# Graph and expert layers on one Trainium2 core: the steps between layers are written tile by tile over three engines, and the member tables become bf16

## The chip, the cores and the metric

The kernel runs on one core of one Trainium2 chip. The time is device microseconds (us) from the start to the end of the program. It was taken three times; the median is the figure that a change is held against. One more execution was recorded by the profiler; every duration below is of that execution.

## The reference

x has 3125 rows of 256 columns. Four pairs of a graph layer and a layer of experts are added to it, each fed with a layer norm of x:

```python
x = x + L0_gnn(layernorm(x), edge_index, edge_weight, ...)   # sums over 100000 edges, then relu(h @ W1 + b1) @ W2 + b2
x = x + L0_ffn(layernorm(x), router_w, w1, b1, w2, b2)       # tokens + the two best of 8 experts, gelu
x = x + L1_gnn(layernorm(x), edge_index, edge_attr_2, ...)   # attention over the edges, 4 heads
x = x + L1_ffn(layernorm(x), Wr, br, ln_g, ln_b, ...)        # router on the rows, experts on layernorm(rows)
x = x + L2_gnn(layernorm(x), W, a_src, a_dst, ..., bias)     # scores (h * a_src).sum per head, softmax per destination
x = x + L2_ffn(layernorm(x), Wg, bg, ...)                    # the two best of 8 experts, relu
x = x + L3_gnn(layernorm(x), W, b, src, dst)                 # three hops
x = x + L3_ffn(layernorm(x), gate_w, gate_b, ...)            # one expert of 8, with a capacity
```

A layer of experts takes logits = rows @ router, picks the best one or two experts for each row, sends the row through them (two products with an activation between) and adds the weighted answers. layernorm subtracts the mean of a row and divides by sqrt(variance + 1e-5).

## The kernel before

x stays in SBUF as 25 tiles of 128 rows, a tile `self.x` of 128 x 25 x 256 f32 (the last tile is partly filled). The stages follow each other as functions: `gcn`, `moe(0)`, `attention`, `moe(1)`, `gat`, `moe(2)`, `hops`, `switch`. The edges were sorted on the chip before. Long loops (the edge sums, the groups of 256 tokens of the experts) fill most of the span. Between two such loops lies a **step between layers**, and this change is about those.

Such a step has up to four parts, each a loop over the 25 tiles. First, x is completed: `gcn` multiplies by W2 (`ps_o`, L1238) and adds to x (L1240); `moe` reads back the experts' answers (`y`) and adds two of them a tile with weights m1 and m2 (L1571); `attention` multiplies its sums by a reciprocal (L1759) and adds them to x (L1760); `gat` does the same from DRAM (loads of `kept` and `sums`, L2259 to L2265). Second, `layernorm` takes bn_stats (L157) and bn_aggr (L160) of each tile on VectorE (DVE), once for each five tiles the root on ScalarE (ACT, L141) and the reciprocal (L142), and then subtracts and multiplies on DVE (L150). Third, `transposed` turns each tile by two transposes on TensorE (PE, L180, tile `ps_tr`), and `copy` takes the result out of PSUM, by turns on ACT (L172) and DVE (L170). Fourth, `logits` multiplies by 8 columns of the router (L1251), or the graph layer multiplies by its weights: attention 136 columns (L1628) and a copy to its table, gat 256 columns (L1866), from which ACT and DVE make two halves of a row (`hr`, L1872, L1873) and a table row `ts` (L1875), and DVE makes the source score by a product with a_src (L1878) and a sum over each head (L1879). In gat one operation then adds the bias to all of x (L1884), and x is written to `kept` (L1886).

Within one straight stretch of code the compiler's scheduler mixes these loops on an engine as it likes; a branch on a value (as in the expert loops) ends a stretch. Only in blocks called `in_order` do instructions of the engines named keep the order in which they are written.

After the logits comes the **routing**: probabilities and the best two (`pair_of_probs`, `pair_of_scores`), then `slots`, which numbers the tokens of each expert and ends in `members`. `members` builds one-hot tables by comparing numbers with `iota` (f32): `sl_ol` with 128 values for each of 25 tiles (L1401) and `sl_oj` with J = 64 values (L1404), multiplied by the tile's number (L1406) and by the partition's (L1408). Tables of the first and the second choice are built one after the other; for each tile one matmul (L1412) multiplies `sl_ol` with `sl_oj`, and `sl_tok` and `sl_to` (L1426) come out: which token sits in which slot. `expert_of` gives each group its expert (`sl_eid`). The experts wait for these. `moe(0)` also adds its normalised rows to x (L1543), and `moe(1)` calls `layernorm` a second time, on the normalised rows, after the logits.

Of the kernel before, what the change touches and what calls it, by code (L numbers as in the profile page):

```python
# [15 lines left out]
OP = mybir.AluOpType  # L16
# [72 lines left out]
class Net:  # L89
# [84 lines left out]
    def transposed(self, src, dst, psum, n=NT):  # L174

        nc = self.nc
        for t in range(n):
            ps = psum.tile([P, 2, P], F32, name="ps_tr", bufs=2)
            for k in range(2):
                nc.tensor.transpose(ps[:, k, :], src[:, t, k * P : (k + 1) * P], self.ident)  # L180
            self.copy(t, dst[:, :, t * P : (t + 1) * P], ps)

# [990 lines left out]
    def gcn_inputs(self):  # L1173
# [4 lines left out]
        if True:  # L1178
# [3 lines left out]
            w2 = keep.tile([P, 2, D], F32, name="w2")  # L1182
            loads.append(nc.sync.dma_start(out=w2, in_=a["L0_gnn_W2"].rearrange("(k p) f -> p k f", p=P)))
# [9 lines left out]
            self.first_inputs = w1, w2, bc, y  # L1193
            self.before_build = {SP: loads, DVE: ready}

    def gcn(self):
        nc, tc = self.nc, self.tc
        w1, w2, bc, y = self.first_inputs
        with self.l0:
            with tc.tile_pool(name="l0h", bufs=1) as hp, \  # L1200
# [3 lines left out]
                gT = hp.tile([P, 2, NT * P], F32, name="hT")  # L1204
# [30 lines left out]
                for t in range(NT):  # L1235
                    ps = psum.tile([P, D], F32, name="ps_o")
                    for f in range(2):
                        nc.tensor.matmul(ps, gT[:, f, t * P : (t + 1) * P], w2[:, f, :],  # L1238
                                         start=f == 0, stop=f == 1)
                    nc.vector.tensor_tensor(self.x[:, t, :], self.x[:, t, :], ps, op=OP.add)  # L1240


    def logits(self, pool, psum, xT, rw, bias):
# [5 lines left out]
        for t in range(NT):  # L1249
            for k in range(2):  # L1250
                nc.tensor.matmul(ps[:, t, :], xT[:, k, t * P : (t + 1) * P], rws[:, k, :],  # L1251
                                 start=k == 0, stop=k == 1)
        if bias is None:
            nc.vector.tensor_copy(lg, ps)
        else:
            bb = pool.tile([P, NE], F32, name="rb")
            nc.sync.dma_start(out=bb, in_=row_bcast(bias, NE))
            nc.vector.tensor_tensor(lg, ps, bb[:, None, :].to_broadcast([P, NT, NE]), op=OP.add)
        return lg
# [60 lines left out]
    def slots(self, pool, keep, psum, oh1, oh2):  # L1320
# [44 lines left out]
        tok, to = self.members(pool, keep, psum, slot, NG)  # L1365
        eid = self.expert_of(pool, keep, first, gf, NG)
        return tok, to, eid
# [14 lines left out]
    def members(self, pool, keep, psum, slot, n):  # L1382

        nc = self.nc
        k = slot.shape[1]

# [7 lines left out]
        ljf = pool.tile([P, 2, k * NT], F32, name="sl_lj")  # L1394
        nc.vector.tensor_copy(ljf, lj)
        ol = pool.tile([P, k * NT, P], BF16, name="sl_ol")
        oj = pool.tile([P, k, NT, 3, J], BF16, name="sl_oj")
        pt = psum.tile([P, 3, J], F32, name="ps_tok", bufs=1)
        for i in range(k):
            h = slice(i * NT, (i + 1) * NT)  # L1400
            nc.vector.tensor_tensor(ol[:, h], self.iota[:, None, :].to_broadcast([P, NT, P]),  # L1401
                                    ljf[:, 0, h, None].to_broadcast([P, NT, P]), op=OP.is_equal)
            o = oj[:, i]
            nc.vector.tensor_tensor(o[:, :, 2, :], self.iota[:, None, :J].to_broadcast([P, NT, J]),  # L1404
                                    ljf[:, 1, h, None].to_broadcast([P, NT, J]), op=OP.is_equal)
            nc.vector.tensor_tensor(o[:, :, 1, :], o[:, :, 2, :],  # L1406
                                    self.iota[:, :NT, None].to_broadcast([P, NT, J]), op=OP.mult)
            nc.vector.tensor_scalar(o[:, :, 0, :], o[:, :, 2, :], self.pidx, None, op0=OP.mult)  # L1408
            if i == 1:
                nc.vector.tensor_scalar(o[:, :, 2, :], o[:, :, 2, :], 2.0, None, op0=OP.mult)  # L1410
            for t in range(NT):
                nc.tensor.matmul(pt.rearrange("p v j -> p (v j)"), ol[:, i * NT + t, :],  # L1412
                                 o[:, t].rearrange("p v j -> p (v j)"),
# [15 lines left out]
    def experts(self, eid, tok, to, xrows, ybuf, pre, b, F, act, usual, scale_shift=None, gated=False):  # L1429
# [7 lines left out]
        with ExitStack() as st:  # L1437
# [61 lines left out]
            for u in range(usual[0]):  # L1499
                group(u)  # L1500
            n = nc.values_load(eid[0:1, usual[-1] :], min_val=0, max_val=usual[-1])
# [26 lines left out]
    def moe(self, layer):  # L1528
        nc, tc, a = self.nc, self.tc, self.a
        with ExitStack() as st:  # L1530

            xp = st.enter_context(tc.tile_pool(name="ex", bufs=1, side="right"))
            xrows, ybuf = self.xrows[layer], self.ybuf[layer]
            with tc.tile_pool(name="exn", bufs=1) as np_, \
                    tc.tile_pool(name="exps", bufs=2, space=PSUM) as psum:
                xn = np_.tile([P, NT, D], F32, name="xn")
                self.layernorm(self.x, xn)
                xT = np_.tile([P, 2, NT * P], F32, name="xT")
                self.transposed(xn, xT, psum)
                if layer == 0:  # L1540
                    lg = self.logits(np_, psum, xT, a["L0_ffn_router_w"], None)
                    m1, oh1, m2, oh2 = self.pair_of_probs(xp, lg)
# [1007 lines left out]
```

## Time and profile before

| what | value |
|---|---|
| median of three runs | 6228.87 us (6225.47 to 6233.80) |
| the profiled execution's own time | 6224.29 us |
| its span, first to last instruction | 6222.4 us |
| mean granted clock of PE | 0.858 |
| PE, DVE, ACT, POOL busy | 79%, 61%, 36%, 39% of the span |
| gcn: last product to logits | 1734 to 1796 us |
| combine after moe(0), attention's table | 1992 to 2051 us |
| attention's finish to logits | 2955 to 3018 us |
| combine after moe(1), gat's table | 3508 to 3611 us |
| gat's finish to logits | 4731 to 4801 us |
| switch: layer norm to logits | 5879 to 5925 us |
| the four routings | 1796 to 1832, 3018 to 3063, 4802 to 4835, 5925 to 5948 us |

Times inside the span count from its start. The profile gives for each engine its busy time; a matmul of f32 counts as two passes, each with a load of weights (PEld) of its own. In the timeline one row is one or several equal instructions on one engine: start, duration, engine, line, operation, what is written and read, and in brackets how long the engine was idle before, and what ended that. A clock of 1.00 is full speed of PE.

### The profile page before, as it was taken

The page shows a single profiled execution, that of the slowest core. Times are in us where ns is not written, and L with a number is a line of the kernel's source. Part 1 is how long each engine was busy: PE and PEld are TensorE (multiplying, and loading weights), DVE is VectorE, ACT ScalarE, POOL GpSimd, SP SyncE. Part 2 cuts the span into 40 slices and gives each one's busy share as a digit, 9 for nine tenths or more (in the row PEclk, how much of TensorE's full clock was granted, in tenths as well). Part 3 has the DMA queues.
Part 4 walks back from the last instruction along what each step waited for, and adds up shares of the span by engine and source line. Part 5 has one row for each costly group of instructions (what it writes and reads, how often), then busy time and mean ns, then how long its engine had stood idle before and what let it go on. Part 6 is the DMA issues. An engine that isn't in the chain of part 4 may idle for free. (4 is left out here: it accounts for less than half of the span.)

```text
span 6222.4 us, 89124 instructions
## 1 busy us (share of the span) xinstructions
PE 4939.7 (79%) x24912; PEld 3986.5 (64%) x24912; DVE 3771.5 (61%) x7790; ACT 2265.3 (36%) x5768; POOL 2425.1 (39%) x2329
## 2 busy tenths in 40 slices
PE   5446787568967888999499579999894899699886
PEld 4335776567855777777488445555554787588765
DVE  6788998681153898999511458888887100532343
ACT  3455776560012113444122166666660222110021
POOL 3778777740015563000022157777770222000021
PEclk8657777668978999999699779999996999899888
DMA  3482334456427574222355377777762554788653
GB/s 87 99 19 36 69 96 108 123 148 166 135 85 215 165 209 143 75 76 68 104 179 184 127 214 196 198 200 198 201 197 74 198 183 143 199 240 239 165 181 126
DMA packets 987149, 912.53 MB, mean 147 GB/s; under 512 B 188419, under 2 KB 897509, under 8 KB 985718
## 3 DMA queue, kind: packets, MB, share of 16 engines
q1 hardware_dynamic: 872098, 711.72, 40.5%
q0 software_dynamic: 84736, 166.99, 11.1%
q10 hardware_dynamic: 29764, 27.47, 1.4%
q8 instruction: 224, 3.67, 0.3%
q14 instruction: 327, 2.68, 0.2%
HBM read 707.87 MB, written 288.94 MB: 160 GB/s over the span
## 5 line engine op out<-in xcount | busy, mean ns | idle before, releaser
L881 POOL DMA_INDIRECT chunks<-tb_pay,tb_row x800 | 981.0, 1226 | 338.5 <-issue 240.2
L242 POOL DMA_INDIRECT g<-table,idx_d x652 | 630.1, 966 | 278.2 <-issue 155.0
L242 POOL DMA_INDIRECT xb<-xrows,sl_tok x172 | 167.4, 973 | 1458.5 <-DVE sl_to L1426 1297.4
L1487 DVE TENSOR_TENSOR yb<-ps_o,eb 128x256 f32<-128x256 f32 x200 | 84.5, 422 | 954.4 <-PE ps_o L1485 935.3
L1478 PE MATMUL ps_h<-xe,ew 128*128 128x256 f32 x2528 | 585.0, 389 | 33.9 <-DVE xe L1472 17.5
L1485 PE MATMUL ps_o<-ew,hT 128*128 128x256 f32 x2528 | 562.5, 379 | 0.0
L1097 DVE SCALAR_TENSOR_TENSOR bk_acc<-bk_acc,bk_on,bk_m 128x256 f32<-128x256 f32 x1102 | 527.5, 479 | 51.8 <-DVE bk_acc L1097 0.4
L1478 PEld LDWEIGHTS ps_h<-xe,ew 128*128 128x128 f32 x2528 | 482.2, 194 | 119.5 <-ACT xe L172 30.3
L1738 PE MATMUL ps_a<-rhs,oh 128*128 128x261 f32 x2208 | 509.9, 387 | 33.3 <-ACT rhs L1735 26.2
L1091 PE MATMUL bk_m<-bk_ow,bk_oh 128*128 128x128 f32 x2208 | 512.2, 372 | 13.1 <-ACT bk_ow L1079 13.1
L2326 PE MATMUL ps_a<-h,m 128*128 128x512 f32 x1875 | 480.4, 406 | 52.6 <-DVE h L2303 52.6
L1485 PEld LDWEIGHTS ps_o<-ew,hT 128*128 128x128 f32 x2528 | 477.5, 190 | 69.1 <-ACT hT L1480 3.9
L1480 ACT ACTIVATE hT<-ps_h,eb 128x256 f32<-128x256 f32 x632 | 296.6, 473 | 582.1 <-PE ps_h L1478 575.5
L1088 PE MATMUL bk_m<-bk_oh 128*128 128x128 f32 x1104 | 304.7, 368 | 243.1 <-DVE bk_acc L1097 224.6
L1738 PEld LDWEIGHTS ps_a<-rhs,oh 128*128 128x128 f32 x2208 | 409.7, 190 | 133.2 <-ACT oh_abs L1723 38.9
L2159 PE MATMUL ps_a<-wt,oh 128*128 128x264 f32 x1664 | 455.4, 421 | 48.3 <-ACT l_iota L2119 25.2
L1079 ACT ACTIVATE bk_ow<-bk_oh,ch 128x128 f32<-128x128 f32 x1104 | 364.1, 390 | 274.1 <-DVE bk_oh L1058 252.0
L1091 PEld LDWEIGHTS bk_m<-bk_ow,bk_oh 128*128 128x128 f32 x2208 | 424.5, 268 | 13.8 <-ACT bk_ow L1079 13.4
L2326 PEld LDWEIGHTS ps_a<-h,m 128*128 128x128 f32 x1875 | 348.0, 189 | 128.9 <-DVE h L2303 58.5
L1088 PEld LDWEIGHTS bk_m<-bk_oh 128*128 128x128 f32 x1104 | 235.9, 264 | 298.6 <-issue 173.1
L2159 PEld LDWEIGHTS ps_a<-wt,oh 128*128 128x128 f32 x1664 | 329.7, 203 | 145.6 <-DVE wt L2149 44.1
L1965 DVE SCALAR_TENSOR_TENSOR tt<-er,col,ps_hd 128x512 f32<-128x512 f32 x416 | 293.2, 743 | 186.7 <-PE ps_hd L1964 169.8
(591 smaller groups left out, 8932.3 us busy)
## 6 DMA issues: line engine op xcount, KB each, us to landing
m<-mats SPq DMA_DIRECT2D x99, 1600.0 KB
mats<-bk_acc SPq DMA_DIRECT2D x1103, 128.0 KB
ew<-in_L_ffn_W_dram SPq DMA_DIRECT2D x116, 1024.0 KB
hd<-rows SPq DMA_DIRECT2D x208, 256.0 KB
stash<-m SPq DMA_DIRECT2D x276, 136.0 KB
ms<-stash SPq DMA_DIRECT2D x276, 136.0 KB
lb<-src_rows SPq DMA_DIRECT2D x276, 128.0 KB
ew<-in_L_ffn_w_dram SPq DMA_DIRECT2D x28, 1024.0 KB
```

Of the source, the lines that this page charges most:

```text
L242: return self.nc.gpsimd.indirect_dma_start(out=out, out_offset=None, in_=table, in_offset=bass.IndirectOffsetOnAxis(ap=idx, axis=0))
L881: sc = nc.gpsimd.indirect_dma_start(out=self.chunks, out_offset=bass.IndirectOffsetOnAxis(ap=self.row[:, k : k + 1], axis=0), in_=self.pay ...
L1079: nc.scalar.mul(ow[:, i], of[:, k % 4 + i, 0, :], ch[:, c + i, 2:3])
L1088: nc.tensor.matmul(ps[:, i, 0, :], oh[:, c0 + i, 0, :], oh[:, c0 + i, 1, :], start=True, stop=True)
L1091: nc.tensor.matmul(ps[:, i, 1, :], of[:, c0 + i, 1, :], ow[:, i], start=True, stop=True)
L1097: nc.vector.scalar_tensor_tensor(new, acc[0], goes_on[:, k + i : k + i + 1], ps[:, i], op0=OP.mult, op1=OP.add)
L1478: nc.tensor.matmul(ps, w1[:, k, f * P : (f + 1) * P], xe[:, k, :], start=k == 0, stop=k == 1)
L1480: nc.scalar.activation(hT[:, f, :], ps, act, bias=b1[:, f : f + 1])
L1485: nc.tensor.matmul(ps, hT[:, f, j * P : (j + 1) * P], w2[:, f, :], start=f == 0, stop=f == FP - 1)
L1738: nc.tensor.matmul(ps, oh[:, c, :], rhs[:, c, :], start=c == 0, stop=c == CH - 1)
L2159: nc.tensor.matmul(po, oh[:, c, :], wt[:, c, :], start=c == 0, stop=c == CH - 1)
L2326: nc.tensor.matmul(pa.rearrange("p i d -> p (i d)"), m[:, j, :], h[:, j].rearrange("p i d -> p (i d)"), start=j == 0, stop=j == NT - 1)
```

## The change

A new function `front(pool, xn, psum, prep, each)` does a whole step between layers in one loop of 34 turns under `in_order(PE, DVE, ACT)`. Turn n completes x for tile n (`prep`), takes its statistics, and each fifth turn the root; five tiles behind, ACT normalises a tile (Identity with a scale and a bias for each row, in place of L150 on DVE) and PE transposes it; six behind, ACT copies the transposes out (all tiles, where before half were DVE's) and `each` multiplies. It is used in six places: by the new `routed` for the layers of experts 0 to 2, with the finish of gcn, attention and gat as `prep`; in attention and gat, with the combine of the layer before as `prep`; and in `switch`, with none. The combine before `hops` stays a plain loop.

In `gcn`, W2 is loaded later, by ACT's queue, into another pool. The addition L1543 is cut into five parts, one after each of the first five groups of experts. The second layer norm of `moe(1)` becomes a factor for each row, worked out from the first one's variance, and 25 multiplications on ACT. In `members` the tables, the numbers compared and the iota are bf16, the last filled once for each routing by ACT (`numbers`), with the tile as the innermost index, so PE reads its operands with a stride of 25 elements; `expert_of` is written before `members`. In `gat`, W gets eight more columns, W times a_src, so that the scores come out of the product; L1878, L1879 and the memset of `ts` for each tile go, a copy of eight columns comes in; the bias is added two tiles at a time in the first 13 steps of gat's edge loop, and `kept` is stored from there by SyncE (SP), five tiles at a time.

```diff
+    def front(self, pool, xn, psum, prep, each):
+        nc, src = self.nc, self.x
+        mv = self.small.tile([P, NT, 2], F32, name="ln_mv")
+        rstd = self.small.tile([P, NT], F32, name="ln_rstd")
+        far = self.small.tile([P, NT], F32, name="ln_far")
+        pts = {}
+        def inverse(t0):
+            r = rstd[:, t0 : t0 + 5]
+            nc.vector.reciprocal(r, r)
+            nc.vector.scalar_tensor_tensor(far[:, t0 : t0 + 5], mv[:, t0 : t0 + 5, 0], -1.0, r,
+                                           op0=OP.mult, op1=OP.mult)
+        with self.in_order(PE, DVE, ACT):
+            for n in range(NT + 9):
+                if n < NT:
+                    if prep is not None:
+                        prep(n)
+                    st = self.small.tile([P, 6], F32, name="ln_st", bufs=4)
+                    nc.vector.bn_stats(st, src[:, n, :])
+                    nc.vector.bn_aggr(mv[:, n, :], st)
+                    if n % 5 == 4:
+                        r = rstd[:, n - 4 : n + 1]
+                        nc.vector.tensor_scalar(r, mv[:, n - 4 : n + 1, 1], 1e-5, 0.0, op0=OP.add, op1=OP.max)
+                        nc.scalar.activation(r, r, AF.Sqrt)
+                if n >= 5 and n % 5 == 0 and n - 5 < NT:
+                    inverse(n - 5)
+                t = n - 5
+                if 0 <= t < NT:
+                    row = pool.tile([P, D], F32, name="ln_x", bufs=3) if xn is None else xn[:, t, :]
+                    nc.scalar.activation(row, src[:, t, :], AF.Identity, scale=rstd[:, t : t + 1],
+                                         bias=far[:, t : t + 1])
+                    pts[t] = psum.tile([P, 2, P], F32, name="ps_tr", bufs=2)
+                    for k in range(2):
+                        nc.tensor.transpose(pts[t][:, k, :], row[:, k * P : (k + 1) * P], self.ident)
+                t = n - 6
+                if 0 <= t < NT:
+                    xT = pool.tile([P, 2, P], F32, name="ln_xT", bufs=3)
+                    nc.scalar.copy(xT, pts.pop(t))
+                    each(t, xT)
+        return mv, rstd
...
+            gp = st.enter_context(tc.tile_pool(name="l0g", bufs=1))
+            gT = gp.tile([P, 2, NT * P], F32, name="hT")
+            w2 = gp.tile([P, 2, D], F32, name="w2")
+            nc.scalar.dma_start(out=w2, in_=a["L0_gnn_W2"].rearrange("(k p) f -> p k f", p=P))
...
+            self.l0.close()
+            outs = st.enter_context(tc.tile_pool(name="l0ops", bufs=2, space=PSUM))
+            def finish(t):
+                ps = outs.tile([P, D], F32, name="ps_o")
+                for f in range(2):
+                    nc.tensor.matmul(ps, gT[:, f, t * P : (t + 1) * P], w2[:, f, :],
+                                     start=f == 0, stop=f == 1)
+                nc.vector.tensor_tensor(self.x[:, t, :], self.x[:, t, :], ps, op=OP.add)
+            self.routed(0, finish)
...
+    def numbers(self, pool):
+        values = pool.tile([P, P, NT], BF16, name="sl_values")
+        self.nc.scalar.copy(values, self.iota[:, :, None].to_broadcast([P, P, NT]))
+        tiles = pool.tile([P, NT], BF16, name="sl_tiles")
+        self.nc.scalar.copy(tiles, self.iota[:, :NT])
+        return values, tiles
+    def members(self, pool, keep, psum, slot, n, numbers):
         nc = self.nc
         k = slot.shape[1]
+        values, tiles = numbers
...
-        ljf = pool.tile([P, 2, k * NT], F32, name="sl_lj")
+        ljf = pool.tile([P, 2, k * NT], BF16, name="sl_lj")
         nc.vector.tensor_copy(ljf, lj)
-        ol = pool.tile([P, k * NT, P], BF16, name="sl_ol")
-        oj = pool.tile([P, k, NT, 3, J], BF16, name="sl_oj")
+        ol = pool.tile([P, k, P, NT], BF16, name="sl_ol")
+        oj = pool.tile([P, k, 3, J, NT], BF16, name="sl_oj")
         pt = psum.tile([P, 3, J], F32, name="ps_tok", bufs=1)
         for i in range(k):
             h = slice(i * NT, (i + 1) * NT)
-            nc.vector.tensor_tensor(ol[:, h], self.iota[:, None, :].to_broadcast([P, NT, P]),
-                                    ljf[:, 0, h, None].to_broadcast([P, NT, P]), op=OP.is_equal)
+            nc.vector.tensor_tensor(ol[:, i], values, ljf[:, 0, None, h].to_broadcast([P, P, NT]), op=OP.is_equal)
             o = oj[:, i]
-            nc.vector.tensor_tensor(o[:, :, 2, :], self.iota[:, None, :J].to_broadcast([P, NT, J]),
-                                    ljf[:, 1, h, None].to_broadcast([P, NT, J]), op=OP.is_equal)
-            nc.vector.tensor_tensor(o[:, :, 1, :], o[:, :, 2, :],
-                                    self.iota[:, :NT, None].to_broadcast([P, NT, J]), op=OP.mult)
-            nc.vector.tensor_scalar(o[:, :, 0, :], o[:, :, 2, :], self.pidx, None, op0=OP.mult)
+            nc.vector.tensor_tensor(o[:, 2], values[:, :J], ljf[:, 1, None, h].to_broadcast([P, J, NT]),
+                                    op=OP.is_equal)
+            nc.vector.tensor_tensor(o[:, 1], o[:, 2], tiles[:, None, :].to_broadcast([P, J, NT]), op=OP.mult)
+            nc.vector.tensor_scalar(o[:, 0], o[:, 2], self.pidx, None, op0=OP.mult)
             if i == 1:
-                nc.vector.tensor_scalar(o[:, :, 2, :], o[:, :, 2, :], 2.0, None, op0=OP.mult)
+                nc.vector.tensor_scalar(o[:, 2], o[:, 2], 2.0, None, op0=OP.mult)
             for t in range(NT):
-                nc.tensor.matmul(pt.rearrange("p v j -> p (v j)"), ol[:, i * NT + t, :],
-                                 o[:, t].rearrange("p v j -> p (v j)"),
+                nc.tensor.matmul(pt.rearrange("p v j -> p (v j)"), ol[:, i, :, t],
+                                 o[:, :, :, t].rearrange("p v j -> p (v j)"),
                                  start=i + t == 0, stop=i == k - 1 and t == NT - 1)
...
+            xn = (np_ if layer else xp).tile([P, NT, D], F32, name="xn")
+            of, whole = self.logits(np_, psum, *(
+                (a["L0_ffn_router_w"], None), (a["L1_ffn_Wr"], a["L1_ffn_br"]), (a["L2_ffn_Wg"], a["L2_ffn_bg"]))[layer])
+            numbers = self.numbers(np_)
+            mv, rstd = self.front(np_, xn, psum, prep, of)
+            lg = whole()
+            m1, oh1, m2, oh2 = (self.pair_of_scores if layer == 2 else self.pair_of_probs)(xp, lg)
+            if layer == 1:
+                again = np_.tile([P, NT], F32, name="ln_again")
+                nc.vector.tensor_tensor(again, mv[:, :, 1], rstd, op=OP.mult)
+                nc.vector.tensor_tensor(again, again, rstd, op=OP.mult)
+                self.rsqrt(again, again, 1e-5, 0.0)
+                for t in range(NT):
+                    nc.scalar.mul(xn[:, t, :], xn[:, t, :], again[:, t : t + 1])
+            for t in range(0, NT, 5):
+                nc.sync.dma_start(out=self.xrows[layer].rearrange("(t p) d -> p t d", p=P)[:, t : t + 5, :],
+                                  in_=xn[:, t : t + 5, :])
+            tok, to, eid = self.slots(np_, xp, psum, oh1, oh2, numbers)
+        self.chosen = st, xn, m1, m2, tok, to, eid
...
+            def between(u):
+                if u < 5:
+                    part = self.x[:, 5 * u : 5 * u + 5, :]
+                    nc.vector.tensor_tensor(part, part, xn[:, 5 * u : 5 * u + 5, :], op=OP.add)
+            self.experts(eid, tok, to, xrows, ybuf, "L0_ffn_w", "L0_ffn_b", 256, AF.Gelu, USUAL_NG, between=between)
...
+        def prep(t):
+            if t % 5 == 0:
+                y = yp.tile([P, 2, 5, D], F32, name="y")
+                for i in range(2):
+                    nc.sync.dma_start(out=y[:, i], in_=of[:, i, t : t + 5, :])
+                ys.append(y)
+            for i, m in enumerate((m1, m2)):
+                nc.vector.scalar_tensor_tensor(self.x[:, t, :], ys[-1][:, i, t % 5, :], m[:, t : t + 1],
+                                               self.x[:, t, :], op0=OP.mult, op1=OP.add)
+        then(prep, st)
...
+                wa = xp.tile([P, 2, D], F32, name="wa")
+                nc.vector.tensor_tensor(wa, w[:, :, :D], av[:, None, :].to_broadcast([P, 2, D]), op=OP.mult)
+                nc.vector.tensor_reduce(w[:, :, D:], wa.rearrange("p k (h f) -> p k h f", h=H), AX.X, OP.add)
+                tss = [xp.tile([P, TW], F32, name=f"ts{i}") for i in range(3)]
+                for ts in tss:
+                    nc.gpsimd.memset(ts, 1.0)
...
-                    nc.vector.memset(tv[:, :, C : C + 1], 1.0)
-                    pr = tp.tile([P, D], F32, name="pr")
-                    nc.vector.tensor_tensor(pr, av, ps, op=OP.mult)
-                    nc.vector.tensor_reduce(ts[:, HW:], pr.rearrange("p (h f) -> p h f", h=H), AX.X, OP.add)
+                    nc.vector.tensor_copy(ts[:, HW:], py[:, D:])
                     nc.sync.dma_start(out=table[t * P : (t + 1) * P, :], in_=ts)
...
-            nc.vector.tensor_tensor(self.x, self.x, bias[:, None, :].to_broadcast([P, NT, D]), op=OP.add)
-            nc.scalar.dma_start(out=kept, in_=self.x)
...
+                def biased(k):
+                    for t in range(2 * k, min(2 * k + 2, NT)):
+                        nc.vector.tensor_tensor(self.x[:, t, :], self.x[:, t, :], bias, op=OP.add)
+                        if t % 5 == 4:
+                            nc.sync.dma_start(out=kept[:, t - 4 : t + 1, :], in_=self.x[:, t - 4 : t + 1, :])
...
+                        if k < 13:
+                            biased(k)
...
+    net.gcn()
+    net.moe(0, net.attention)
+    net.moe(1, net.gat)
+    net.moe(2, net.hops)
+    net.switch()
```

## The prediction

> **What bounds the kernel now.** I read the page first. No engine is full: PE is busy 79% of the span, at a granted clock that sinks again and again.
>
> ```profile
> PE 4939.7 (79%) x24912; PEld 3986.5 (64%) x24912; DVE 3771.5 (61%) x7790; ACT 2265.3 (36%) x5768; POOL 2425.1 (39%) x2329
> PEclk8657777668978999999699779999996999899888
> ```
>
> The change leaves the long loops alone, so I took the windows between them (columns: window, sum, then busy us of PE, PEld, DVE, ACT, POOL, clock, DMA share, GB/s).
>
> ```profile
> 1734.00:1757.00 23.00, 22.57 (x108) 19.23 (x106) 21.08 (x81) 2.10 (x7) 0.00 (x0) 1.00 0.00 1
> 1757.00:1796.00 39.00, 30.52 (x150) 29.24 (x150) 20.75 (x48) 6.33 (x15) 0.00 (x0) 0.55 0.25 85
> 2955.00:2972.00 17.00, 0.00 (x0) 0.00 (x0) 16.96 (x52) 0.00 (x0) 0.00 (x0) 0.52 0.00 0
> 2972.00:3018.00 46.00, 31.27 (x150) 30.28 (x150) 29.18 (x123) 7.27 (x20) 0.00 (x0) 0.50 0.05 15
> 3018.00:3063.00 45.00, 7.93 (x54) 6.83 (x54) 42.11 (x143) 2.48 (x6) 0.00 (x0) 0.55 0.17 58
> 4802.00:4835.00 33.00, 7.98 (x54) 6.86 (x54) 28.27 (x72) 1.51 (x2) 0.00 (x0) 0.58 0.00 0
> ```
>
> Here one part follows the other: in 2955–2972 DVE alone works (attention's finish), then PE walks through transposes and logits at half clock, then DVE alone again (routing). Nothing of the next stage runs meanwhile, so all of it is on the path. The timeline shows why PE isn't busy sooner:
>
> ```profile
> 4772.70 0.40 DVE L170 COPY xT<-ps_tr 128x256 f32<-128x256 f32 x1
> 4773.11 0.39 DVE L170 COPY xT<-ps_tr 128x256 f32<-128x256 f32 x1
> 4773.16 1.12 PE L180 MATMUL ps_tr<-ident,xn 128*128 128x128 f32 x4 [8.72 <-DVE xT L170]
> 4774.08 1.70 DVE L150 TENSOR_SCALAR xn<-x,ln_mv,ln_rstd 128x256 f32<-128x256 f32 x5
> 3555.68 6.82 DVE L1884 TENSOR_TENSOR x<-x,bias 128x6400 f32<-128x6400 f32 x1
> 3562.88 0.71 PEld L180 LDWEIGHTS ps_tr<-ident,xn 128*128 128x128 f32 x4 [5.40 <-DVE xT L170]
> ```
>
> PE waits for copies that stand in DVE's queue behind statistics and normalisation, and in gat's step behind the bias addition. In the groups of the first routing the table building is the largest part:
>
> ```profile
> L1401 DVE TENSOR_TENSOR sl_ol<-iota,sl_lj 128x3200 bf16<-128x3200 f32 x2 | 6.9, 3474 | 0.0
> L1406 DVE TENSOR_TENSOR sl_oj<-sl_oj,iota 128x1600 bf16<-128x1600 bf16 x2 | 3.6, 1806 | 0.0
> L1404 DVE TENSOR_TENSOR sl_oj<-iota,sl_lj 128x1600 bf16<-128x1600 f32 x2 | 3.6, 1800 | 0.0
> L1408 DVE TENSOR_SCALAR sl_oj<-sl_oj,pidx 128x1600 bf16<-128x1600 bf16 x2 | 1.3, 632 | 0.0
> ```
>
> **The steps, one by one.** Durations: on DVE a 128x256 product or sum takes 0.42, combine 0.48, bn_stats 0.43, bn_aggr 0.17; a dependent one starts about 0.04 after the end, an independent one about 0.08 before. On ACT a copy takes 0.37 (L172); Identity with two per-row operands isn't in the trace. Its nearest row is L1480 (bias per row, 128x256): 0.47; below it lies the copy's 0.37, and I take 0.47. PE's 256-column pass takes 0.22 at clock 1.00 and 0.44 cold (mean of L1866), a transpose or 8-column pass 0.21 cold, and warm 0.12 (an estimate: four transposes took 1.09 cold and, in attention's step at 2038 us, 0.65 warm). Every pipelined step also pays about 7 us at its end: five tiles of lag at 0.84 of ACT (4.2), a root and reciprocal (0.5), the last transposes and logits (about 2).
>
> 1. gcn (1734 to 1795.7, 62 us). PE does per tile four passes of L1238 (0.87), two transposes and four logit passes. They are now between products that keep the clock at 1.00, so six at 0.12: 1.6 a tile, DVE's dependent sum, statistics and aggregate (0.46+0.47+0.11) beside it. 25 x 1.6 and 6 of end = 46: gain 16. If the clock stays at 0.5, 25 x 3.0 + 6 = 81: loss 19. With a shorter end at best 18. I take the warm end, since PE was at 1.00 in the first window with the same products.
> 2. attention's table (1992.5 to 2050.8, 58 us). DVE: two combines 1.02, stats 0.47, aggregate 0.11, root's share 0.12, half a table copy 0.2: 1.93 x 25 = 48, end 8, and twice some 2 us where DVE's table copy waits for PE behind a fresh group. 60; gain 0, between -8 and +8.
> 3. attention's finish to logits (2955 to 3018, 63 us). DVE: 0.46+0.46+0.47+0.11+0.12 = 1.62 x 25 = 41, end 7: gain 15 (8 to 20). PE's 1.23 cold fits under it.
> 4. gat's table (3508 to 3611, 103 us). ACT is a loop here: norm 0.47, copy 0.37, then it waits for its product (four passes: 1.12 warm, 1.75 cold; 1.6 taken), hr 0.37, ts 0.38: 3.2 x 25 = 80. Each fifth turn it waits for DVE, whose `hr` difference stood behind ACT: 5 x 1.5. End 7. 95: gain 8 (-5 to +28). The bias addition (6.8) and L1878, L1879 (0.82 a tile) leave DVE, where they aren't the bound any more. On SP's queue the next `y` loads stand behind the stores of `hr` and `ts`, which wait for ACT; three `y` buffers of five tiles cover that (else the 6 us that one load of `y` takes, at the start).
> 5. gat's finish to logits (4730.7 to 4801.4, 71 us). As 3 with the reciprocal of five tiles (0.12 a tile): 1.74 x 25 = 44, end 7, first loads 3: gain 17 (10 to 22). Loads are 6.6 MB at the 209 GB/s of that window, 1.26 us a tile, under DVE's pace.
> 6. switch (5879 to 5925, 46 us). No `prep`: PE cold at 1.23 x 25 = 31, start 3.5, end 2.5: gain 9 (4 to 12).
> 7. The second layer norm. Routing 1 takes 45 us, routings 0 and 2 take 36 and 33; the 25 multiplications on ACT (10 us) lie beside DVE's `slots`, and the stores of rows behind them end before the tables do: gain 10 (5 to 11). If that cover is gone, the stores' 7.5 us come on the path.
> 8. Tables. All operands of L1401, L1404, L1406 become 16-bit. L1406 has one f32 operand and costs as much as L1404 with f32 throughout (1.81, 1.80); L1408, bf16 and a scalar, takes a third. I take halving: 3.47+1.80+1.81 less a routing, 7.1. Against it stands PE reading with a 50-byte stride: the 25 second matmuls (2.22 us) are behind the tables, and could cost 0 to 5 more. Net 4 for three routings, 1 for the switch's half: 13 (0 to 24). The ACT copies that fill 3200 values (3.6 by L1607, 128x2960 in 3.57) lie in ACT's idle start.
> 9. At nothing: the five additions in moe(0) (1.4 each; DVE is busy 36 of 158 us there, POOL 111 and PE 126; uncovered 7); W2's load (during the products); the eight columns of W (two operations before the loop); `expert_of` earlier, since all four first weight loads were issued 0.2 us after `sl_to` ended, in the first routing 4.5 us after `sl_eid` (0 to 6 better). In gat's loop 25 bias additions and five stores on SP's queue come before its `hd` loads; DVE idles about 1.3 of each 3 us of an early turn, so -1, or -11 if all is uncovered. The switch's `numbers` fill may lie before its tables: -1 to -4.
>
> The Trainium skill speaks against step 8: "SBUF — State Buffer", the note on cachelines, says lines have 16 bytes and bf16 strides past 8 elements lose bandwidth, so 25 would. The nearest row, transposes L1602 of a stride of 20 bytes, took 435 ns against 432 of contiguous L180; no penalty there. By the rule the sum would be up to 5 us a routing worse, as in the bound above.
>
> For the tables "VectorE: DVE Perf Modes" (the perf-mode tier table) gives two-tensor operations 2x when all is bf16; no row of before has such an operation, and by the rule the term is the 7.1 above.
>
> **The sum.** 16+0+15+8+17+9+10+13-2 = 86. The profiled execution took 6224.3, so 6138 for such a one; the median stands 4.6 above it: 6143.
>
> **Rivals.**
> (a) The in-order lists cost more than their slowest engine: the product in step 1 stays cold (-19 for +16), step 4 gains nothing, the strided reads eat half of step 8. Then 86-35-8-6 = 37: about 6192. For it: clock 0.50 in all logit windows. Against: these windows had PE waiting, as shown.
> (b) More: products warm in step 4 (2.7 a tile, +12), step 2 +8, early expert numbers +6 twice, strides free (+9): 127, about 6102. For it: PE's clock was 0.75 in 2017–2051.
> (c) Slower: each turn becomes a chain. ACT's norm waits for DVE, PE for ACT, ACT's copy for PE, and DVE's next `prep` for the turn before. The whole chain is 1.6+0.47+0.43+0.37+0.85 = 3.7. My turns sum to 11.3 over the six steps (1.9 each) and my ends and extra waits to 55; so the six steps (403 us before) and the 21 of points 7 to 9 break even at (403+21-55)/150 = 2.46 a turn. At 2.6 the loss is 21: 6250. Against: the five-tile lag is there for DVE to run ahead, and only steps 2 and 4 hand something back to DVE.
> (d) The change doesn't do what it says: Identity makes ACT load a table each time it follows the root. 1.28 (ACT_TABLE_LOAD) x 2 x 5 groups x 6 steps = 77, half of it hidden under DVE: gain 48, 6181. Against: copies and roots alternate in every step before with one load at its start.
>
> **How the numbers follow.** Forecast 0.55, (a) 0.17, (b) 0.10, (c) 0.10, (d) 0.06; 0.02 remains for no difference. What a measurement of this kernel can tell from no change is about 0.2%, 12 us. Range: (b)'s 6102, less 12 for its own spread, to just above (a), 6090 to 6205; it leaves out (c) and the ends. Chances: faster 0.87, same 0.03, slower 0.10.
>
> **What would show it.** Right: gcn's step under 50 us at a clock near 1.0; 3 and 5 at a DVE period of 1.6–1.75 without gaps; L1401's successor near 1.75 us; routing 1 as short as routing 0. Wrong: ACT_TABLE_LOAD repeated in a step; DVE waiting in each turn for PE or ACT; matmuls of `ps_tok` well over 0.09 apart; PE waits in gat's first 13 turns on DVE's bias additions.

## The result, and the profile after

The changed kernel takes 6274.31 us (median; 6265.39 to 6277.26) against 6228.49 of the kernel before: a ratio of 1.007, 95% interval [1.0053, 1.0088]. It is slower, by 46 us. The prediction said 6143. The profiled execution of the changed kernel has a span of 6275.4 us, 53 longer than before, at a mean clock of 0.849. Of the runs below, x8, x9 and x10 were taken while the kernel before took 7051.37 us (the mean clock of x8 is 0.795), so they are read by their ratios to it and by stretches whose unchanged neighbours kept their times (attention's finish to logits: 47.5 in x8, 47.6 in x9).

The busy shares of the span have hardly changed: PE 80% for 79%, DVE 59% for 61%, ACT 38% for 36%.

So the answer lies again in the steps between the layers. From the traces' start times (logits: start of the copy or sum that writes `lg`; routing: from there to the start of `sl_to`):

| stretch | before | after | gain predicted | gain measured |
|---|---|---|---|---|
| 1 gcn: last edge product to logits | 83.0 | 101.3 | 16 | -18.3 |
| 2 attention: first combine to its finish | 962.7 | 984.3 | 0 | -21.6 |
| 3 attention's finish to logits | 62.6 | 47.5 | 15 | 15.1 |
| 4 gat: first combine to last table store | 102.8 | 135.4 | 8 | -32.6 |
| 5 gat's finish to logits | 70.1 | 73.0 | 17 | -2.9 |
| 6 switch: last hop's sum to logits | 46.4 | 35.4 | 9 | 11.0 |
| 7, 8 the four routings | 35.1, 44.9, 32.8, 22.1 | 40.5, 41.1, 38.1, 22.1 | 23 | -6.9 |
| 9 all else | | | -2 | 3.2 |

The last column sums to -53.0; its line 9 is what remains between the two spans. Three losses stand in single steps (1, 2, 4), one in the routings, and step 5 got nothing out of nearly the same code that won 15 in step 3. The windows of the changed kernel (columns as before: busy us of PE, PEld, DVE, ACT, POOL, then the clock, DMA share and GB/s):

```profile
1734.00:1752.20 18.20, 12.92 (x69) 10.20 (x69) 11.71 (x38) 7.59 (x14) 0.00 (x0) 1.00 0.02 6
1752.20:1813.00 60.80, 47.83 (x184) 39.31 (x182) 23.62 (x62) 19.05 (x45) 0.00 (x0) 0.58 0.15 53
2999.00:3047.00 48.00, 30.84 (x149) 29.61 (x150) 37.79 (x124) 26.79 (x62) 0.00 (x0) 0.50 0.01 1
3533.00:3668.00 135.00, 61.71 (x150) 37.24 (x150) 53.95 (x165) 40.59 (x108) 1.27 (x3) 0.50 0.33 113
4791.00:4864.00 73.00, 30.96 (x150) 29.71 (x150) 39.14 (x124) 22.25 (x55) 0.00 (x0) 0.50 0.38 125
```

In 2999–3047 DVE is busy 38 of 48 us: the step runs at its slowest engine. In 3533–3668 no engine is busy even half the time, at half clock: that is a chain, not a bound. In gcn's step the clock is 1.00 at first and 0.58 from 1752.2 on. In 4791–4864 DVE does what it did in 2999–3047 and takes 25 us longer.

### The profile page after: what moved, and what is told of

Same layout as the page of the kernel before. It is cut to its first block, busy times and chain, and to the rows that moved or that the text cites. A ratio compares the mean times of both kernels' runs of the same rounds, so it can differ in the third digit from the quotient of the medians.

```text
span 6275.4 us, 89407 instructions
## 1 busy us (share of the span) xinstructions
PE 5023.0 (80%) x24912; PEld 4019.5 (64%) x24912; DVE 3686.4 (59%) x7497; ACT 2381.4 (38%) x6018; POOL 2428.3 (39%) x2332
## 5 line engine op out<-in xcount | busy, mean ns | idle before, releaser
L1543 ACT ACTIVATE hT<-ps_h,eb 128x256 f32<-128x256 f32 x632 | 296.5, 473 | 573.1 <-PE ps_h L1541 565.3
```

The source lines that it names most:

```text
L1543: nc.scalar.activation(hT[:, f, :], ps, act, bias=b1[:, f : f + 1])
```

## The experiments

Each changes the changed kernel in one place, but for the combinations. The kernel before took 6227.34 us beside x1 to x4 and 6221.1 beside x5 to x7 and x11. Ratios are to the kernel before in the same session.

**The tables.** In the groups of the first routing of the changed kernel DVE's operations did halve, but the 50 matmuls take 17.0 us. Each lasts 515 ns and they overlap; their starts are 0.337 us apart:

```profile
L1474 PE MATMUL ps_tok<-sl_oj,sl_ol 128*128 128x192 bf16 x50 | 17.0, 515 | 12.6 <-DVE sl_oj L1470 12.6
L1474 PEld LDWEIGHTS <-sl_ol 128*128 128x128 bf16 x50 | 7.3, 145 | 22.2 <-issue 13.4 <-DVE sl_ol L1465 8.9
L1465 DVE TENSOR_TENSOR sl_ol<-sl_values,sl_lj 128x3200 bf16<-128x3200 bf16 x2 | 3.7, 1872 | 0.0
L1467 DVE TENSOR_TENSOR sl_oj<-sl_values,sl_lj 128x1600 bf16<-128x1600 bf16 x2 | 2.0, 1004 | 0.0
```

x1_tables takes the tables of before:

```diff
-        ol = pool.tile([P, k, P, NT], BF16, name="sl_ol")
-        oj = pool.tile([P, k, 3, J, NT], BF16, name="sl_oj")
+        ol = pool.tile([P, k * NT, P], BF16, name="sl_ol")
+        oj = pool.tile([P, k, NT, 3, J], BF16, name="sl_oj")
...
-                nc.tensor.matmul(..., ol[:, i, :, t], o[:, :, :, t].rearrange("p v j -> p (v j)"), ...)
+                nc.tensor.matmul(..., ol[:, i * NT + t, :], o[:, t].rearrange("p v j -> p (v j)"), ...)
```

> The changed kernel with the member tables as before (f32 compares, contiguous operands for TensorE), all else as changed. If the strided operands cost what the tables' step lost, the matmuls of ps_tok are 0.09 us apart again instead of 0.34, DVE's compares take 3.47 and 1.80 us instead of 1.87 and 1.00, and routings 0 and 2 (logits to sl_to) go from 40.5 and 38.1 us to about 35.2 and 32.7: some 16 us less in all, about 6258. Rival: the routing is longer for another reason (the earlier expert_of, weight loads beside it): then it stays at 38 to 40.

Measured: routings 35.3, 36.0, 32.9, 22.3; 6262.04 us, ratio 1.0056 [1.0034, 1.0079]. The strided reads cost what the theory said. Routing 1 is now as short as routing 0, 8.9 less than before: the gain of the second layer norm, which the tables had hidden.

x2_moving parts the two operands:

```diff
-        oj = pool.tile([P, k, 3, J, NT], BF16, name="sl_oj")
+        oj = pool.tile([P, k, NT, 3, J], BF16, name="sl_oj")
-            nc.vector.tensor_tensor(o[:, 2], values[:, :J], ljf[:, 1, None, h].to_broadcast([P, J, NT]), ...)
+            nc.vector.tensor_tensor(o[:, :, 2, :], ramp[:, None, :J].to_broadcast([P, NT, J]),
+                                    ljf[:, 1, h, None].to_broadcast([P, NT, J]), op=OP.is_equal)
```

> The changed kernel with only sl_oj, TensorE's moving operand, laid out contiguously again (bf16, tile number outside, J innermost, the compared number broadcast along it); sl_ol, the stationary operand, keeps its stride of 50 bytes. If the moving operand alone pays for its stride, ps_tok's matmuls are about 0.09 us apart, and routing 0 falls from 40.5 to 27 to 30 us, under the 35.2 of before; if the weight loads pay too, they stay above 0.2 apart and the routing above 33. For DVE: if a broadcast innermost operand still lets two-tensor operations run at the bf16 rate, the compares of 1600 stay at 1.00 us; if not, they go back to 1.80 and the routing is 3 us longer.

The groups of its first routing:

```profile
L1477 PE MATMUL ps_tok<-sl_oj,sl_ol 128*128 128x192 bf16 x50 | 6.2, 299 | 15.1 <-DVE sl_oj L1473 14.3 <-DVE sl_oj L1475 0.8
L1477 PEld LDWEIGHTS <-sl_ol 128*128 128x128 bf16 x50 | 6.1, 153 | 15.6 <-DVE sl_ol L1467 8.9 <-issue 6.7
L1469 DVE TENSOR_TENSOR sl_oj<-sl_ramp,sl_lj 128x1600 bf16<-128x1600 bf16 x2 | 3.6, 1802 | 0.0
```

In the kernel before the same matmuls are:

```profile
L1412 PE MATMUL ps_tok<-sl_oj,sl_ol 128*128 128x192 bf16 x50 | 6.1, 295 | 18.3 <-DVE sl_oj L1408 17.3 <-DVE sl_oj L1410 1.0
```

With the moving operand contiguous the 50 matmuls are back at 6.2 us for 6.1, though the stationary one still has its 50-byte stride: only the moving operand pays. But a compare whose operand is broadcast along the innermost axis takes 1802 ns, bf16 or not. Routings 32.0, 32.6, 29.6, 20.7, about 20 less than before in all, and 6254.20 us (1.0047 [1.0028, 1.0067]); the 27 to 30 expected for the first was missed by DVE's 1.80.

x8_stride5 asks how much stride is free:

```diff
-        oj = pool.tile([P, k, 3, J, NT], BF16, name="sl_oj")
+        oj = pool.tile([P, k, 5, 3, J, 5], BF16, name="sl_oj")
-                                 o[:, :, :, t].rearrange("p v j -> p (v j)"),
+                                 o[:, t // 5, :, :, t % 5].rearrange("p v j -> p (v j)"),
```

> The changed kernel with sl_oj in groups of five tiles: the tile number within a group is innermost, so TensorE's moving operand has a stride of 5 elements (10 bytes) instead of 25 (50 bytes), and the compares run along five equal-spaced 16-bit elements; sl_ol keeps its stride of 50 bytes. If TensorE pays for leaving a 16-byte line with each element, 10 bytes cost little: matmuls of ps_tok 0.09 to 0.2 apart, and with the compares still at 1.00 us routing 0 falls from 40.5 to 27 to 31, below the 32.0 of the contiguous operand. Rival: any stride costs: 0.34 apart, routing 0 at 38 to 41. Rival for DVE: rows of five break the bf16 rate: 1.80 instead of 1.00, then 31 to 33.

In its first routing there is a matmul each 0.217 us (49 weight loads in 10.61 us). The compares took 1.14 us. Routings 34.9, 35.5, 32.4, 20.8: the first three are 2.9 longer than x2's; ratio 1.0035 [1.0024, 1.0045].

The matmuls' spacing must be read with the clock beside it. In x2's first routing the first 25 start mostly 0.160 us apart, at a clock of 0.56 over the group, and the second 25 at 0.082, at 1.00. The strided ones ran at 0.50 throughout, in the changed kernel and in x8. At one clock, 0.50, the strides can be compared in the fourth routing, whose 25 matmuls have 96 columns; in order x2 (contiguous), x8 (10 bytes) and the changed kernel (50 bytes):

```profile
5968.40:5970.70 2.30, 2.16 (x25) 1.96 (x24) 0.05 (x2) 0.00 (x0) 0.00 (x0) 0.50 0.00 0
...
6785.20:6788.40 3.20, 2.98 (x25) 2.73 (x24) 0.13 (x2) 0.00 (x0) 0.00 (x0) 0.50 0.04 10
...
5997.30:6001.90 4.60, 4.46 (x25) 3.50 (x24) 0.05 (x1) 0.00 (x0) 0.00 (x0) 0.50 0.01 2
```

So the stride itself costs 1.4 times at 10 bytes and 2.1 times at 50. The rest of the loss in the other routings is the clock: 50 strided matmuls, 17 us on end, left it at 0.50, while 25 contiguous ones, busy 4 us, were followed by 1.00 in the first three routings of x2. Why is not shown. The Trainium skill ("SBUF — State Buffer", the cacheline note) would let 8 bf16 elements pass free of loss; these runs agree that 25 cost, but here 5 cost too, and the measurement decides.

**gat's finish.** One group in the timeline of the changed kernel (root on ACT, the load of sums issued by ACT's queue, the reciprocal's input on DVE):

```profile
4801.86 0.21 ACT L208 ACTIVATE ln_rstd<-ln_rstd 128x5 f32<-128x5 f32 x1 [11.28 <-DVE ln_rstd L207]
4801.86 0.39 ACTq L2346 DMA_DIRECT2D acc<-sums  x1
4806.01 0.20 DVE L2349 TENSOR_SCALAR l_rec<-acc 128x40 f32<-128x40 f32 x1 [4.18 <-DMA acc<-sums]
```

A DMA that ACT issues is an instruction of ACT, so `in_order` holds it too: the load for the next five tiles is issued behind the root of these, and DVE waits 4 to 5 us in each group. x3_acc_sp:

```diff
-                        nc.scalar.dma_start(out=acc.rearrange("p t h f -> p t (h f)"),
+                        nc.sync.dma_start(out=acc.rearrange("p t h f -> p t (h f)"),
```

> The changed kernel with the loads of sums in gat's finish issued by SyncE instead of ScalarE, so that they are not in the order of ScalarE's work. Theory: each load waits in ScalarE's list behind the root of the group before, and DVE then waits 4 to 5 us a group for it; without that the groups come 8.7 us apart instead of 13.4, and gat's finish to logits falls from 73 to 50 to 55 us. Rival: the loads are bound by bandwidth, or on SyncE stand behind the stores of xrows, which wait for rows: then groups stay over 12 us apart and the step over 68.

DVE's waits for that load (us in total, times, longest), first in the changed kernel, then in x3:

```profile
DVE l_rec L2349 <- DMA acc<-sums: 23.4, 5, 5.4
```

```profile
DVE l_rec L2349 <- DMA acc<-sums: 7.4, 1, 7.4
```

The wait that is left is for the first load, before the stretch begins. The step takes 50.2 us, 19.9 less than in the kernel before; 6255.95 us, ratio 1.0040 [1.0020, 1.0060]. Settled.

**gat's table.** One turn of the changed kernel:

```profile
3600.35 0.60 ACT L214 ACTIVATE ln_x<-x,ln_far,ln_rstd 128x256 f32<-128x256 f32 x1
3600.85 0.36 ACT L222 COPY ln_xT<-ps_tr 128x256 f32<-128x256 f32 x1
3601.00 0.69 PE L218 MATMUL ps_tr<-ident,ln_x 128*128 128x128 f32 x2 [1.87 <-ACT ln_x L214]
3601.49 1.96 PE L1949 MATMUL ps_y<-w,ln_xT 128*128 128x264 f32 x4
3603.53 0.37 ACT L1956 CAST hr<-ps_y 128x256 fp32r<-128x256 f32 x1 [2.32 <-issue]
3603.94 0.42 DVE L1957 TENSOR_TENSOR hr<-ps_y,hr 128x256 fp32r<-128x256 f32 x1 [1.70 <-ACT hr L1956]
3604.39 0.37 ACT L1959 COPY ts<-ps_y 128x256 f32<-128x256 f32 x1 [0.49 <-DVE hr L1957]
3604.66 0.60 ACT L214 ACTIVATE ln_x<-x,ln_far,ln_rstd 128x256 f32<-128x256 f32 x1
```

From one norm to the next 4.31 us, and each line waits for one above it: the transposes for the norm, the product, behind them in PE's list, for them, `hr` for the product. Two turns in each five take 6.6: there ACT waits for DVE's part of root and reciprocal as well. x4_drain lets the turn's product be emptied in the next turn:

```diff
+                    def drain():
                     ps = py[:, :D]
...
                     nc.sync.dma_start(out=table[t * P : (t + 1) * P, :], in_=ts)
+                    return drain
...
-                    each(t, xT)
+                    drains[t] = each(t, xT)
+                if drains.get(n - 7) is not None:
+                    drains[n - 7]()
```

> The changed kernel with the work on a tile's product (hr, ts, the eight scores, attention's table copy) written one turn later than the product, so that ScalarE and DVE need not wait in their lists for a product of the same turn. Theory: gat's table is one chain a turn (norm 0.5, copy 0.36, product 2.25, hr 0.4, difference 0.45, ts 0.27 = 4.3); with the product out of it the turn falls to what DVE or PE need, 2.5 to 3.0, and the step (first combine to last table store) from 135 to 75 to 90 us. Attention's step from 65 (first to last combine) to 50 to 57. Rival: TensorE at half clock is the bound by itself (transposes 0.43, four passes 1.75 and gaps): then a turn stays over 3.3 and the step over 95.

The window of its step, to be read beside 3533–3668 above:

```profile
3510.00:3594.00 84.00, 47.02 (x150) 31.06 (x150) 52.83 (x166) 39.34 (x109) 1.27 (x3) 0.70 0.53 181
```

The step falls to 83.7 us, attention's stretch to 961.2 (its combines from 65.6 to 49.3 us), the time to 6206.83, ratio 0.9968 [0.9952, 0.9984]: this alone makes the change pay. With the chain broken PE is busy 56% of the step instead of 46% and its clock is 0.70 instead of 0.50. In attention's table DVE's waits for the product of its own turn, in the changed kernel

```profile
DVE table L170 <- PE ps_y L1703: 25.6, 11, 3.9
```

come to 7.3 us in x4; in the kernel before they were 5.8.

x9_order asks about `ts`, which began 0.04 us after the difference had ended though it needs nothing of it:

```diff
                     nc.scalar.copy(hr[:, 0, :], ps)
+                    nc.scalar.copy(tv[:, :, :C], ps.rearrange("p (h f) -> p h f", h=H))
                     nc.vector.tensor_tensor(hr[:, 1, :], ps, hr[:, 0, :].bitcast(F32), op=OP.subtract)
...
-                    nc.scalar.copy(tv[:, :, :C], ps.rearrange("p (h f) -> p h f", h=H))
```

> The changed kernel with one line moved: in gat's table ScalarE's copy ts is written before DVE's difference, not after it. In the changed kernel ts began 0.04 us after the difference had ended, in every turn, though it reads nothing that the difference writes. Theory: the readers of one product in PSUM are released in the order written, so the difference (0.45) is a link of the chain of a turn: a turn falls from 4.32 to about 3.85, and gat's step from 135 to 122 to 126. Rival: ts waits for something else (an older store of its tile): then the turn stays at 4.3 and the step at 135.

The step takes 123.6 instead of 135.4 us (x8, from the same session and with the code of the changed kernel here, 135.5; ratio 1.0038 [1.0022, 1.0053]): the difference was a link of the chain by its place in the text. In x9 it is the difference that starts 0.03 us after `ts` has ended. That readers of one PSUM tile follow each other in the order written fits; by which rule they do was not tried.

**gcn's step.** The first two holes in PE's work in the changed kernel:

```profile
1743.06 0.44 PE L218 MATMUL ps_tr<-ident,xn 128*128 128x128 f32 x2 [2.70 <-ACT xn L214]
1751.08 0.44 PE L218 MATMUL ps_tr<-ident,xn 128*128 128x128 f32 x2 [2.13 <-ACT xn L214]
```

The first left the clock at 1.00; it fell at 1752.2, 1.1 us after the second. It came up twice more in this step and fell again at 1789.7 and 1806.8, 0.6 and 1.4 us after holes of 2.13. In the same place the scheduler had put an addition of moe(0) (`x<-x,xn`, 1.49 us of DVE behind a wait for ACT's rows): it stands in the same stretch of code and is free to move. x6_hoist ties it behind `sl_to`, x5_slack gives more lag:

```diff
+                    self.behind(one, self.placed, "after the routing")      # x6_hoist
```

```diff
-                        nc.scalar.activation(r, r, AF.Sqrt)
-                if n >= 5 and n % 5 == 0 and n - 5 < NT:
-                    inverse(n - 5)
-                t = n - 5
+                if n >= 5 and n % 5 == 0 and n - 5 < NT:
+                    nc.scalar.activation(r, r, AF.Sqrt)
+                if n >= 6 and n % 5 == 1 and n - 6 < NT:
+                    inverse(n - 6)
+                t = n - 7
```

> The changed kernel with the five additions of x and xn in the first experts tied behind the routing's last operation, so that the scheduler can't put them into gcn's step. Theory: the scheduler put them there, each 1.49 us of DVE behind a wait for ScalarE's rows, in the fifth turn, and this opened the holes in which TensorE's clock fell: without them gcn's step falls from 101 to 65 to 85 us, and the experts stay at 162. Rival: the holes of the fifth turn are there anyway: then the step falls by no more than 5 to 8, the additions' own time.

> The changed kernel with two more tiles of lag: ScalarE takes the root one turn later, DVE the reciprocal one turn after that, and the norm runs seven tiles behind instead of five, the copies eight. Theory: each fifth turn of every step is a chain through DVE, ScalarE and TensorE, because root, reciprocal and norm follow each other without a turn between, and the holes in TensorE's work keep its clock low; with the lag gcn's step (last product to logits) falls from 101 to 70 to 85 us, attention's table by 5 to 10, while the step after attention's sums, where DVE is the bound, gets 1 to 3 longer. Rival: the clock is low whatever the holes and gcn's step is bound by TensorE at 3.0 a tile: then it stays over 92.

x6: 98.6 us, within the 95.9 to 101.3 that this step takes in the five kernels with the same code there; 6270.44 us, ratio 1.0083 [1.0063, 1.0104]. Its second hole, and the window from the fall of its clock on:

```profile
1749.18 0.44 PE L218 MATMUL ps_tr<-ident,xn 128*128 128x128 f32 x2 [2.13 <-ACT xn L214]
...
1750.40:1808.00 57.60, 44.93 (x183) 37.36 (x181) 17.03 (x56) 18.79 (x45) 0.00 (x0) 0.62 0.16 56
```

The theory of the moved addition falls; its rival holds. x5:

```profile
1733.00:1786.00 53.00, 44.78 (x254) 37.12 (x254) 34.33 (x98) 26.21 (x61) 0.00 (x0) 0.95 0.19 63
```

gcn's step 74.7 us at a clock of 0.95, 8.3 less than in the kernel before; attention's stretch 960.9, gat's table 119.7; 6200.12 us, ratio 0.9974 [0.9962, 0.9986]. The lag decides: PE's waits for ACT in the step fall from 17.5 to 7.4 us and the longest hole from 2.7 to 1.6, and the clock stays up. So some 10 of the 26.6 us gained are the waits themselves, and the rest goes with the clock (an estimate from these two figures). That the holes bring the clock down is argued from their order in time and from x5, which changes the holes by changing the lag; no run changes a hole alone.

**Together.** x7_all holds x2, x3, x4, x5 and x6; x10_best takes x8 for x2 and adds x9; x11_final is x7 and x9.

> The changed kernel with the contiguous moving operand, sums loaded by SyncE, products drained a turn later, two more tiles of lag, and the additions behind the routing. If the five causes are separate and each is what the theories say, the sum of their gains (routings 25 to 40, gat's finish 18 to 23, tables 50 to 70, gcn's step 16 to 35) takes the time from 6274 to about 6110 to 6165, faster than 6228 before. Rival: they are the same loss seen twice, or TensorE's clock bounds all steps: then it ends between 6180 and 6230.

6115.98 us, ratio 0.9834 [0.9818, 0.9851]; gcn 75.2, gat's table 73.6, gat's finish 51.4, routings 32.1, 32.6, 29.6, 20.6.

> The combination of before (sums loaded by SyncE, products drained a turn later, two more tiles of lag, the additions behind the routing) with the moving operand at a stride of 5 elements in place of the contiguous one, and with ts before the difference. If both single runs go as their theories say, three routings get 3 to 4 us shorter and gat's table 0 to 8 us than in the combination before (6116 us): 6098 to 6112. If the stride costs, it is 15 to 25 slower than that.

6931.05 us against 7051.37, ratio 0.9826 [0.9809, 0.9842]. gat's table 65.0, but the routings 34.9, 35.5, 32.5: what one edit gave the other took.

> The first combination (contiguous moving operand, sums loaded by SyncE, products drained a turn later, two more tiles of lag, the additions behind the routing) with ts before the difference as the only addition. From the stages of the single runs: gat's table 73.6 to about 65, the routings as in the first combination (32.1, 32.6, 29.6); so 8 to 9 us less than it, a ratio to the kernel before of about 0.982 against 0.9834. Rival: the shorter table step is given back in the edge loop that follows it: then the ratio is 0.983 to 0.984.

6108.78 us against 6221.13, ratio 0.9824 [0.9808, 0.9841], with gat's table at 65.1 and the routings of x7: 1.8% faster than the kernel before, and by the two ratios (0.9824 and 1.007) 2.4% faster than the changed one. Against x7 the ratios' intervals overlap; the spans differ by 9.5 us (6106.1 and 6115.6), the 8.5 of gat's table and little else.

## Why the prediction was wrong

The forecast priced each step by its slowest engine and a fixed end. Where the lists had slack, this held. It failed in the claim, made against rival (c), that the lag lets DVE run ahead and "only steps 2 and 4 hand something back to DVE", and in the price of what these two hand back. Of the 139 us between the gain of 86 that was forecast and the loss of 53 in the profile, 97 lie in steps 1, 2 and 4, where turns became chains as (c), held at 0.10 and 6250 us, has it. Another 20 lie in step 5 (who issues a load) and 30 in the routings (the stride); the rest came out 7 better.

- **Steps 3 and 6 were right**: 15.1 and 11.0 measured for 15 and 9. A turn of step 3 took 1.55 us (7.76 for five tiles) for 1.62. Here the slowest engine is handed almost nothing back: DVE waits 0.3 us in all for the root in step 3; in step 6 it waits 9.5 for it, but there PE is the slowest, and its one wait, 5.8 for the first row, lies at the start.
- **Step 1 failed in its clock term.** "The six are now between products that keep the clock at 1.00" took PE's density for given. The named other end, -19, is what came (-18.3), by luck in part: a tile cold took the 3.0 of that sum (2.99, 1758.91 to 1761.90, the starts of two of DVE's sums), but only six of the 24 turns were so; seven with a hole took 3.5 to 5.4 and the others 1.0 to 2.4. The step also handed work back, against the claim in (c) that only 2 and 4 do: DVE's sum waits for PE's `ps_o`, which stands behind transposes that wait for ACT, which waits for DVE. x5 moved the end to +8.3, still half of the 16.
- **Step 2** failed in its wait: 0 predicted, bound -8, measured -21.6. "Twice some 2 us where DVE's table copy waits for PE" was 25.6 us in 11 waits. With the drains the stretch gains 1.5, with the lag 1.8 (waits 7.3 and 10.7); each alone breaks the loop. Together (x7) they make 7.4, so the two cures overlap for the most part. The stretch is long: in the kernels with the code of the changed one it takes 979.8 to 987.9, so a us or two says little.
- **Step 4 failed in three terms of the turn**: the product 2.3 with its handover and the two transposes ahead of it (1.6 taken; 1.75 was the cold end), the norm 0.60 long, 0.50 start to start (0.47 taken, from L1480), and the difference between `hr` and `ts`, 0.45, which I had put on DVE beside ACT. 4.3 for 3.2, at 25 turns 28 us. The fifth turns cost more too: eight turns are 2.25 longer than the others, 18 us, for the 7.5 taken. -32.6 lay far below the bound of -5.
- **Step 5 failed by an overlooked wait.** I weighed the loads' bandwidth and not who issues them. Cured by one word (x3), the step gains 19.9 for the predicted 17.
- **Step 7 was right** (8.9 in x1 for 10). **Step 8 failed in the stride's price**: 6.4 of DVE was saved for the 7.1 said (3.47 went to 1.87 and 1.80 to 1.00; per routing 3.2+1.6+1.6), but DVE's wait for the matmuls rose from 2.31 to 13.95 us, 11.6 more where I had allowed 0 to 5. The nearest row that I chose, f32 transposes at 20 bytes, was no measure: the strided tile `ch` is loaded there as the stationary operand (the last of L1602's weight loads has the 72 columns of the last chunk, its moving operand still 128), and x2 shows that the stationary operand's stride is nearly free. The 2.22 us for the second 25 held at a clock of 1.00, and I took the first 25 to stay hidden: at 0.337 and a clock of 0.50, 50 matmuls are 16.9 us. Of the two strides, x2 keeps the one of `sl_ol`, with its gain of 3.2 on DVE.
- **Step 9 was nearly right**: 3.2 us for -2, a remainder that holds the spread between two executions too. gat's loop was 2.5 longer with the bias in it. The weight loads of the first routing began 22 us before `sl_to` (1831.26 and 1853.23), 0.5 after `sl_eid`; in the kernel before, the profile has them waiting 3.1 us for `sl_to`. So no pool held them, and the place of `expert_of` in the text goes with it, though no run moves that alone. It brought nothing there (experts 162.4 for 161.7).
- **Rival (d)** didn't occur: at most one table load at a step's start, and none at the turn from root to Identity.

## What to carry to other kernels

When loops are merged into one list in written order, draw one turn's arrows through all engines, DMAs included that a computing engine issues: each arrow that returns to an engine in the same turn adds to the turn, and a turn of lag or of drain took most of that away here. Price a TensorE part of such a turn at the low clock unless nothing can open a hole in it. Before a table is turned for VectorE's sake, look at who reads it along the other axis, and as which operand.

## What the runs showed of the hardware

- At a granted clock of 0.50, bf16 matmuls with a moving operand of 192 columns, each with its load of weights, start 0.160 us apart contiguous (x2), 0.217 at a stride of 10 bytes (x8) and 0.337 at 50 (changed kernel). Contiguous at 1.00 they start 0.082 apart; no strided one ran at 1.00.
- A stationary operand at 50 bytes hardly costs: a load takes 153 ns for 118 in the first routing (x2 and the kernel before), and the 50 matmuls 6.2 us for 6.1.
- DVE's compares run at 1.00 us for 1600 bf16 elements, at 1.14 in rows of five, and at 1.80 if one operand is broadcast along the innermost axis.
- Inside gcn's step the granted clock was 0.95 where the longest hole before a transpose was 1.6 us (x5), and 0.58 to 0.62 from the second hole on where holes of 2.1 came again and again (changed kernel, x6). It does not follow PE's busy time alone: 17 us of strided matmuls without a hole ran at 0.50.
